# A four-layer graph kernel: empty GAT list places skipped, their factors cleared, and another pace for the tails

## The chip, the cores and the metric

The kernel runs on one core of a Trainium2 chip. The metric is the device time of one execution in microseconds (us), as the median of several runs. The kernel before took 3423.61 us (three runs, 3417.87 to 3426.96).

## The reference

Eight batches of a graph of 2,048 nodes with 128 features, and one adjacency matrix for all. Two layers of graph attention with eight heads and a feed-forward part come first, then two GAT layers. A GAT layer, shortened:

```python
h = x @ W
s_i, s_j = h @ a_src, h @ a_dst
e = s_i[:, :, None] + s_j[:, None, :]
e = jnp.where(e >= 0, e, NEG_SLOPE * e)
e = jnp.where(adj[None] == 0, -jnp.inf, e)
out = jnp.einsum('bij,bjd->bid', jax.nn.softmax(e, axis=-1), h)
x = layer_norm(out + x)
```

The adjacency has a density of 1/128, so a node has 16 neighbours on average; the inputs used have 32,733 edges, and a node has 4 to 30 of them. The kernel gathers the neighbours' rows and never forms the full score matrix.

## The kernel before

Nodes are sorted by their number of neighbours and cut into 16 tiles of 128 nodes, one node to a partition. Tile t has a list of neighbours for each node, padded to `CAPS[t]` places (28 and 2 "folded" ones for tile 0, down to 11 for tile 15; 277 in all). An empty place holds the index 2,048 (`far` in `find_lists`).

For each layer there is a table in DRAM with one row for each node. In the two attention layers (0 and 1) a row holds keys and values, 8,192 bytes. In the GAT layers (2 and 3) it holds the eight batches' features `h` and, behind them, two factors for each batch, the exponentials of `s_j` and of 0.2 `s_j`: 1,040 floats, 4,160 bytes. The GAT tables have one row more, row 2,048, which is all zeros. `gather` (L319) fetches the rows of one list place of a tile by an indirect DMA that POOL issues; an index above the bound is skipped by it. In the attention layers index 2,048 is above the bound; in the GAT layers it fetches the zero row, whose factors of zero make the place count for nothing.

The list places are worked through in chunks: two places to a chunk in the attention layers, up to four in the GAT layers (75 chunks in each). Six buffers `kv0` to `kv5` hold the gathered chunks in turn. `fetch` (L1096) issues gathers up to three or four chunks ahead, as soon as the needed part of the table has been written. `put[l]` counts the tiles whose rows are in table `l`; the first chunks of a layer use lists sorted so that they don't need the last three tiles.

A GAT chunk (`gat_chunk`, L736) works in stages: VectorE computes the weights from the two factors (L753 to L759) into PSUM and into `ws`; VectorE scales six of the eight batches (L765) and ScalarE two (L770); VectorE adds the halves of the chunk (L774); PE sums the places into `acc` (L780). When a tile has all its chunks, `outputs` divides, and a tail (`gat_tail`, or `attention_tail` in two halves) adds the residual, normalises, and projects into the next layer's rows. The squares are ScalarE's (L479, L817), the power is POOL's (L484, L844), the scaling with it is ScalarE's again (L488, L825). The rows go into the next table by an indirect scatter (`put_rows`, L502), the last layer's into the output (L862).

The order of instructions on every engine is written out by hand with Python generators. `slot()` is called three times for each chunk, and moves every list-building thread and every tail on by one stage, then calls `fetch`. In some places it moves the tails on once more:

```python
def hurry():
    c = every[min(now[0], len(every) - 1)]
    return c["l"] == 2 and c["t"] == NT - 1 or c["l"] > 1 and put[c["l"]] < NT
...
    beat[0] += 1
    if beat[0] % 3 == 0 and hurry():
        advance(tails)
```

So at every third slot there is an extra stage while the last tile of layer 2 is at work, and while a GAT layer runs whose own table isn't complete.

Of the kernel before, what the change touches and what calls it, by code (L numbers as in the profile page):

```python
# [8 lines left out]
F32 = mybir.dt.float32  # L9
# [8 lines left out]
P = 128  # L18
B, N, D = 8, 2048, 128
NT = N // P  # L20
# [8 lines left out]
NB = 8  # L29
CHUNK = 4 * NB * (D + 2)  # L30
KVB = 6
# [51 lines left out]
def sparse_path(ctx: ExitStack, tc: tile.TileContext, ins: dict, out: bass.AP, flag: bass.AP):  # L83
# [10 lines left out]
    nc = tc.nc  # L94
    const = ctx.enter_context(tc.tile_pool(name="const", bufs=1))
    work = ctx.enter_context(tc.tile_pool(name="work", bufs=2))
    small = ctx.enter_context(tc.tile_pool(name="small", bufs=2))
    dram = ctx.enter_context(tc.tile_pool(name="dram", bufs=1, space=bass.MemoryType.DRAM))
# [4 lines left out]
    def misc():  # L103
        return pm.tile([P, 512], F32, tag="m", name="m")
# [9 lines left out]
    nc.vector.tensor_scalar_add(center, ident, -1.0 / P)  # L114
    onesc = const.tile([P, 1], F32, name="onesc")
    nc.vector.memset(onesc, 1.0)
    half = const.tile([P, 8], F32, name="half")
    nc.vector.memset(half, -0.5)

# [21 lines left out]
    bufs = [const.tile([P, CHUNK], F32, name=f"kv{i}") for i in range(KVB)]  # L141
    turn = [-1]

    def buffer():
        turn[0] += 1
        return bufs[turn[0] % KVB]
# [155 lines left out]
    def width(l):  # L302
        return NB * (2 * D if l < 2 else D + 2)


    tables = [dram.tile([N + (l > 1), width(l)], F32, name=f"table{l}") for l in range(4)]

    x_rows = ins["x_nodes"]

# [9 lines left out]
    def gather(l, index, dst):  # L319
        nc.gpsimd.indirect_dma_start(  # L320
            out=dst, out_offset=None, in_=tables[l][:, :],
            in_offset=bass.IndirectOffsetOnAxis(ap=index, axis=0),
            bounds_check=N - (l < 2), oob_is_err=False,
        )

    def transpose4(src):
# [115 lines left out]
    def folded_sums(w, box):  # L442

        columns = w.shape[-1]
        ps = misc()[:, :columns]
        for i in range(FOLD):
            nc.tensor.matmul(ps, merge, w[:, i, :], start=i == 0, stop=i == FOLD - 1)
        box["folded"] = small.tile([P, columns], F32, tag="folded", name="folded", bufs=1)
        nc.scalar.copy(box["folded"], ps)
# [283 lines left out]

    def gat_chunk(l, c):  # L736
        box, t, k, ns = c["box"], c["t"], c["k"], c["ns"]
        mine = own[:, t, :]
        if c["folded"]:
            pf = misc()[:, :NB]  # L740
            nc.tensor.matmul(pf, spread, mine, start=True, stop=True)
            mine = small.tile([P, NB], F32, tag="mine", name="mine", bufs=1)
            nc.scalar.copy(mine, pf)
            yield
        if k == 0:
            box["acc"] = pacc.tile([P, NB // 4, 512], F32, tag="acc", name="acc")
            at, n = (0 if t % 2 == 0 else 512 - NB * CAPS[t]), CAPS[t]
            box["w"] = pair[:, at : at + NB * n].rearrange("p (s b) -> p s b", b=NB)
        acc, w = box["acc"], box["w"]
        hs = c["buf"]  # L750
        wc = w[:, k : k + ns, :]
        wa, wb = hs[:, :, NB * D : NB * (D + 1)], hs[:, :, NB * (D + 1) :]
        nc.vector.tensor_mul(wb, wb, mine[:, None, :].to_broadcast([P, ns, NB]))  # L753
        nc.vector.tensor_max(wc, wa, wb)
        if c["folded"]:
            box["wf"] = small.tile([P, FOLD, NB], F32, tag="wf", name="wf", bufs=1)
            nc.vector.tensor_max(box["wf"], wa, wb)
        ws = small.tile([P, 4, SCALED], F32, tag="ws", name="ws", bufs=3)
        nc.vector.tensor_max(  # L759
            ws[:, :ns, :], wa[:, :, NB - SCALED :], wb[:, :, NB - SCALED :]  # L760
        )
        yield
        hv = hs[:, :, : NB * D].rearrange("p s (b c) -> p s b c", b=NB)
        nv = NB - SCALED
        nc.vector.tensor_mul(  # L765
            hv[:, :, :nv, :], hv[:, :, :nv, :], wc[:, :, :nv, None].to_broadcast([P, ns, nv, D])
        )
        for i in range(ns):
            for b in range(nv, NB):
                nc.scalar.mul(hv[:, i, b, :], hv[:, i, b, :], ws[:, i, b - nv : b - nv + 1])  # L770
        yield
        left = -(-ns // 2)
        if ns > 1:
            nc.vector.tensor_add(hv[:, : ns - left], hv[:, : ns - left], hv[:, left:ns])  # L774
        yield
        if c["folded"]:
            folded_sums(box["wf"], box)
        for i in range(left):
            for j in range(NB // 4):
                nc.tensor.matmul(  # L780
                    acc[:, j, :], merge if c["folded"] else ident, hv[:, i, 4 * j : 4 * j + 4, :],
                    start=k + i == 0, stop=c["last"] and i == left - 1,
                )
        yield
# [85 lines left out]
    def start():  # L870
# [173 lines left out]
        next(weights, None)  # L1044
        for i in (3, 4, 5):
            nc.scalar.copy(bufs[i], nil.to_broadcast([P, CHUNK]))
        for l in (2, 3):
            nc.sync.dma_start(tables[l][N : N + 1, :], bufs[5][:1, : width(l)])


    def verdict():
# [26 lines left out]
    put = [NT, 0, 0, 0]  # L1078
    every = []
    blocks = [[{} for _ in range(NT)] for _ in range(4)]  # L1080
    for l in range(4):
        per = 2 if l < 2 else 4
        for t, k, ns, folded in pieces(l, per):
            c = dict(l=l, t=t, k=k, ns=ns, folded=folded, box=blocks[l][t])
            c["last"] = not folded and k + ns == (CAPS[t] if t > 0 else BASE)
            c["run"] = (attention_chunk if l < 2 else gat_chunk)(l, c)
            every.append(c)
    now = [0, 0]
    beat = [0]

    def advance(group):
        for g in list(group):
            if next(g, 0) == 0:
                group.remove(g)

    def fetch():  # L1096

        while now[1] < len(every):
            c = every[now[1]]
            l, t, k, ns = c["l"], c["t"], c["k"], c["ns"]  # L1100

            if now[1] - now[0] > (4 if now[1] >= KVB and every[now[1] - KVB]["l"] > 1 else 3):
                return
            resorted = l > 0 and t < 2 and not c["folded"]
            need = NT - max([b for end, b in EARLY[t] if k + ns <= end] + [0] if resorted else [0])
            if put[l] < need:
                return
            c["buf"] = buffer()[:, : ns * width(l)].rearrange("p (s c) -> p s c", s=ns)
            for i in range(ns):
                at = t * BASE if resorted else first[t]  # L1110
                index = (sorted_lists if resorted else lists)[:, at + k + i : at + k + i + 1]
                gather(l, index, c["buf"][:, i])
            now[1] += 1

    def hurry():

        c = every[min(now[0], len(every) - 1)]
        return c["l"] == 2 and c["t"] == NT - 1 or c["l"] > 1 and put[c["l"]] < NT

    def slot():  # L1120
        advance(threads)
        advance(tails)
        fetch()
        beat[0] += 1
        if beat[0] % 3 == 0 and hurry():
            advance(tails)

    def drain():
# [40 lines left out]
    def layers():  # L1169
        state(0, 0)  # L1170
        drain()
        fetch()
        begin(every[0])
        for _ in weights:
# [3 lines left out]
        for i in range(len(every) + 2):  # L1178
            now[0] = i
            fetch()  # L1180
            c2, c1, c, n1, n2 = (chunk(i + j) for j in range(-2, 3))
            if c["k"] == 0:
                l, t = c["l"], c["t"]
                if l == 0:
                    if t + 2 < NT:
                        threads.append(find_lists(t + 2))
                    if t == 0:
                        state(0, 1)
                        threads.append(later(12, lambda: state(0, 2) or iter(())))
                        threads.append(later(12, clear_late))  # L1190
                    if t in (2, 6):
                        threads.append(order_lists(t // 4))
                while l < 2 and "asked" not in c["box"]:
                    slot()
            while i < len(every) and now[1] <= i:
                slot()
# [11 lines left out]
            if c1["l"] in (2, 3) and c1["last"]:  # L1208
                sums(c1["l"], c1["t"], c1["box"])
            go(c)  # L1210
            slot()
            go(c)
            slot()
# [10 lines left out]
    with tc.manual_schedule():  # L1224
        start()
        layers()
# [521 lines left out]
```

## Time and profile before

| | |
|---|---|
| median of the runs | 3423.61 us |
| profiled execution: its own time | 3428.05 us |
| its span in the trace | 3426.3 us |
| busy PE, VectorE, ScalarE, POOL | 2761.3, 3051.6, 1425.1, 2229.1 us |
| DMA | 200,625 packets, 986.52 MB |
| first VectorE work of layer 2, first gathers of layer 3's complete table | 2223 us, 2884 us |

Busy time of an engine is the time in which it executes; a DMA instruction of POOL counts while POOL issues it, not while the data move. The DMA share is the mean busy share of the core's 16 DMA engines. A wait is put down to what ended it. In the names of groups, `kv<-table,lists` is a gather into one of the six buffers, `kv<-table,sorted_lists` the same with the sorted lists of tiles 0 and 1, and L320 is the line in `gather` that issues it.

### The profile page before, as it was taken

Reading aid. Unit: us, or ns where it says so; the run is one execution under the profiler, and the core shown is the slowest. Engines: PE = TensorE matmul, PEld = TensorE weight load, DVE = VectorE, ACT = ScalarE, POOL = GpSimd, SP = SyncE. Lnnn points to the kernel's source line nnn. Section 1 sums busy time; section 2 is a strip of 40 time slices with the busy share of each in tenths; the row PEclk is TensorE's granted clock in tenths of the full one; section 3 lists DMA queues with packets and bytes.
Section 4 is the critical chain, followed back from the end, with each engine's and each line's share of the span. In section 5 each row is a group of like instructions: output and inputs, shape, how many; then the busy total and the mean of one; then the engine's idle time right before and its main releaser. Section 6 shows DMA issues by size and latency. Waiting matters only on the chain.

```text
span 3426.3 us, 34767 instructions
## 1 busy us (share of the span) xinstructions
PE 2761.3 (81%) x10618; PEld 1595.4 (47%) x10618; DVE 3051.6 (89%) x2807; ACT 1425.1 (42%) x4972; POOL 2229.1 (65%) x1453
## 2 busy tenths in 40 slices
PE   5657888788899996888889899976888986767775
PEld 4523445455555652545455555553444543333332
DVE  8799999999999989999999999947867866889885
ACT  4712333334344441333334344453545654445444
POOL 0065888687667654566677666637767865788773
PEclk9888999999999999999999999998988998888887
DMA  8697778888878777677888888658988986899873
GB/s 326 201 355 275 284 283 303 307 303 301 312 290 296 277 287 280 238 309 284 335 298 292 315 297 295 241 171 307 326 290 311 352 326 214 291 313 334 304 275 118
DMA packets 200625, 986.52 MB, mean 288 GB/s; under 512 B 31918, under 2 KB 33712, under 8 KB 128436
## 3 DMA queue, kind: packets, MB, share of 16 engines
q0 software_dynamic: 175024, 890.45, 72.2%
q1 hardware_dynamic: 20502, 75.52, 5.9%
q10 hardware_dynamic: 4904, 18.24, 1.7%
q8 instruction: 87, 1.43, 0.2%
q14 instruction: 108, 0.88, 0.1%
HBM read 937.16 MB, written 91.55 MB: 300 GB/s over the span
## 4 chain that ended last, share of the span: by engine, by line
DVE 36%; PE 23%; issue 19%; DMA 11%; POOL 4%; ACT 4%; POOLq 0%; ACTq 0%; DVEq 0%; another core or an unknown queue 0%
DVE kv L614 13%; DVE kv L628 13%; PE acc L780 7%; PE acc L638 5%; DMA kv<-table,lists 4%; POOL kv L320 3%; DVE sc L617 3%; DMA kv<-table,sorted_lists 2%; DVE kv L774 2%; PE m L329 2%; DVE kv L765 2%; DMA table<-rows,perm 1%; DMA xs<-in_x_nodes_dram,perm 1%; PE m L720 1%; DVE w L459 1%
## 5 line engine op out<-in xcount | busy, mean ns | idle before, releaser
L320 POOL DMA_INDIRECT kv<-table,lists x955 | 1463.0, 1532 | 381.6 <-issue 203.6
L638 PE MATMUL acc<-kv,ident 128*128 128x512 f32 x2200 | 1109.0, 634 | 221.8 <-DVE kv L628 221.3
L780 PE MATMUL acc<-kv,ident 128*128 128x512 f32 x1184 | 622.2, 679 | 190.9 <-DVE kv L774 157.7
L638 PEld LDWEIGHTS acc<-kv,ident 128*128 128x128 f32 x2200 | 413.1, 201 | 652.7 <-issue 365.9
L617 DVE TENSOR_REDUCE sc<-kv 128x128 f32<-128x2048 f32 (+1 forms) x284 | 634.0, 2233 | 9.2
L628 DVE TENSOR_TENSOR kv<-kv,w 128x2048 f32<-128x2048 f32 (+1 forms) x284 | 631.5, 2223 | 8.6 <-ACT w L623 7.9
L614 DVE TENSOR_TENSOR kv<-kv,q 128x2048 f32<-128x2048 f32 (+1 forms) x282 | 629.2, 2231 | 10.7 <-DMA kv<-table,sorted_lists 5.7
L780 PEld LDWEIGHTS acc<-kv,ident 128*128 128x128 f32 x1184 | 248.9, 220 | 514.4 <-issue 294.8
L765 DVE TENSOR_TENSOR kv<-kv,pair 128x3072 f32<-128x3072 f32 (+1 forms) x150 | 466.2, 3108 | 1.0
L484 POOL TENSOR_TENSOR rs<-ss,half 128x4 f32<-128x4 f32 x128 | 222.8, 1741 | 313.9 <-ACT n L479 313.0
L774 DVE TENSOR_TENSOR kv<-kv 128x2048 f32<-128x2048 f32 (+1 forms) x150 | 296.1, 1974 | 145.9 <-ACT kv L770 137.0
L770 ACT ACTIVATE kv<-kv,ws 128x128 f32<-128x128 f32 x1108 | 339.0, 406 | 175.2 <-DVE ws L759 108.9
L479 ACT ACTIVATE n<-m,eps 128x128 f32<-128x128 f32 x512 | 181.0, 366 | 423.6 <-PE m L720 212.5
L623 ACT ACTIVATE w<-sc,lmask 128x64 f32<-128x64 f32 x554 | 165.1, 352 | 443.8 <-DVE sc L617 425.5
L320 POOL DMA_INDIRECT kv<-table,sorted_lists x153 | 203.5, 1330 | 114.8 <-PE acc L638 45.9
L488 ACT ACTIVATE n<-m,rs 128x128 f32<-128x128 f32 x512 | 146.0, 370 | 124.4 <-POOL rs L484 124.2
L502 POOL DMA_INDIRECT table<-rows,perm x57 | 102.5, 1798 | 129.1 <-ACT rows L553 33.2
L329 PE MATMUL m<-ident,n 128*128 128x128 f32 x640 | 105.2, 287 | 67.3 <-ACT n L825 47.4
L720 PE MATMUL m<-w_L_w,hT 128*128 128x128 f32 x1024 | 156.6, 275 | 1.7 <-ACT hT L704 1.7
L329 PEld LDWEIGHTS m<-ident,n 128*128 128x128 f32 x640 | 82.4, 147 | 132.6 <-ACT n L825 57.6
L720 PEld LDWEIGHTS m<-w_L_w,hT 128*128 128x128 f32 x1024 | 135.2, 192 | 1.9 <-ACT hT L704 1.9
L699 PE MATMUL m<-n1T,w_L_gnn_W 128*128 128x512 f32 x256 | 131.6, 597 | 0.8 <-ACT n1T L694 0.4
(242 smaller groups left out, 3476.4 us busy)
## 6 DMA issues: line engine op xcount, KB each, us to landing
kept<-xT SPq DMA_DIRECT2D x48, 512.0 KB
xT<-kept SPq DMA_DIRECT2D x48, 512.0 KB
kv<-in_adj_dram SPq DMA_DIRECT2D x16, 1024.0 KB
table<-kv ACTq DMA_DIRECT2D x16, 1024.0 KB
kv<-table,lists POOLq DMA_INDIRECT x955
kv<-in_x_nodes_dram SPq DMA_DIRECT2D x16, 512.0 KB
kv<-table,sorted_lists POOLq DMA_INDIRECT x153
found<-cand POOLq DMA_DIRECT2D x16, 64.0 KB
```

The source lines that it names most:

```text
L320: nc.gpsimd.indirect_dma_start(out=dst, out_offset=None, in_=tables[l][:, :], in_offset=bass.IndirectOffsetOnAxis(ap=index, axis=0), bound ...
L329: nc.tensor.transpose(pt[:, j * P : (j + 1) * P], src[:, j, :], ident)
L484: nc.gpsimd.tensor_tensor(rs, ss, half[:, :4], op=ALU.pow)
L614: nc.vector.tensor_mul(kk, kk, q[:, None].to_broadcast([P, ns, NB, D]))
L617: nc.vector.tensor_reduce(sc[:, :ns].rearrange("p s (b h) -> p (s b) h", h=NH), kk.rearrange("p s b (h j) -> p (s b) h j", h=NH), axis=AX. ...
L628: nc.vector.tensor_mul(vv, vv, w[:, k : k + ns, :].rearrange("p s (b h) -> p (s b) h", h=NH)[:, :, None, :] .to_broadcast([P, ns * NB, HD, ...
L638: nc.tensor.matmul(acc[:, j, :], merge if c["folded"] else ident, kv[:, i, 4 * j : 4 * j + 4, D:], start=k + i == 0, stop=c["last"] and i ...
L720: nc.tensor.matmul(y[:, j, :], hT[:, f, j, :], wt["2"][:, f, :], start=False, stop=f == 1, skip_group_check=True,)
L765: nc.vector.tensor_mul(hv[:, :, :nv, :], hv[:, :, :nv, :], wc[:, :, :nv, None].to_broadcast([P, ns, nv, D]))
L770: nc.scalar.mul(hv[:, i, b, :], hv[:, i, b, :], ws[:, i, b - nv : b - nv + 1])
L774: nc.vector.tensor_add(hv[:, : ns - left], hv[:, : ns - left], hv[:, left:ns])
L780: nc.tensor.matmul(acc[:, j, :], merge if c["folded"] else ident, hv[:, i, 4 * j : 4 * j + 4, :], start=k + i == 0, stop=c["last"] and i = ...
```

## The change

The gathers of the GAT layers get the same bound as the others, so an empty place moves no row; the row of zeros and its two loads go. What is then in the buffer at such a place is what the chunk before left there. So that it counts for nothing, its factors have to be zero: after a GAT chunk's scalings ScalarE writes zeros over the factors of all four places of the buffer, and for the first six chunks of layer 2, whose buffers come from an attention layer, POOL does so ahead of the gathers. Features that are left over are then multiplied by a weight of zero.

The second part is the tails' pace. There is an extra stage at every slot, but only while layer 2 is at work and its own table (`put[2]`) is incomplete; at the last tile of layer 2 and at the start of layer 3 there is none.

```diff
+    nought = const.tile([P, 1, 1], F32, name="nought")
+    nc.vector.memset(nought, 0.0)
...
-    tables = [dram.tile([N + (l > 1), width(l)], F32, name=f"table{l}") for l in range(4)]
+    tables = [dram.tile([N, width(l)], F32, name=f"table{l}") for l in range(4)]
...
-            bounds_check=N - (l < 2), oob_is_err=False,
+            bounds_check=N - 1, oob_is_err=False,
...
+    def gat_weights(buf):
+        return buf[:, : 4 * width(2)].rearrange("p (s c) -> p s c", s=4)[:, :, NB * D :]
...
                 nc.scalar.mul(hv[:, i, b, :], hv[:, i, b, :], ws[:, i, b - nv : b - nv + 1])
+        nc.scalar.copy(gat_weights(c["whole"]), nought.to_broadcast([P, 4, 2 * NB]))
         yield
...
-        for l in (2, 3):
-            nc.sync.dma_start(tables[l][N : N + 1, :], bufs[5][:1, : width(l)])
...
-            c["buf"] = buffer()[:, : ns * width(l)].rearrange("p (s c) -> p s c", s=ns)
+            c["whole"] = buffer()
+            c["buf"] = c["whole"][:, : ns * width(l)].rearrange("p (s c) -> p s c", s=ns)
+            if l == 2 and every[now[1] - KVB]["l"] == 1:
+                nc.gpsimd.memset(gat_weights(c["whole"]), 0.0)
...
-    def hurry():
-        c = every[min(now[0], len(every) - 1)]
-        return c["l"] == 2 and c["t"] == NT - 1 or c["l"] > 1 and put[c["l"]] < NT
...
-        beat[0] += 1
-        if beat[0] % 3 == 0 and hurry():
+        if now[0] < len(every) and every[now[0]]["l"] == 2 and put[2] < NT:
             advance(tails)
```

More of the change, by code (lines that the diff above doesn't have):

```diff
@@ L1088, in sparse_path @@
     now = [0, 0]
-    beat = [0]
     def advance(group):
```

## The prediction

> **What bounds the kernel now.** I read the busy shares by stage first, then the groups of the two GAT layers, then who waited for whom there, then the DMA counts. The first chunk of the third layer starts on VectorE at 2223 us and the program ends at 3426 us, so the change can act on some 1,206 us. Busy time in five stretches (columns: length, PE, PEld, DVE, ACT, POOL with their counts, PE clock, DMA share, GB/s):
>
> ```profile
> 2220.00:2320.00 100.00, 70.17 (x327) 44.68 (x325) 47.59 (x45) 45.25 (x171) 39.77 (x36) 0.89 0.50 166
> 2320.00:2795.00 475.00, 398.47 (x1408) 222.37 (x1408) 385.49 (x412) 248.92 (x969) 349.59 (x272) 0.89 0.91 322
> 2795.00:2890.00 95.00, 64.50 (x250) 38.45 (x250) 48.43 (x46) 41.25 (x163) 47.73 (x37) 0.82 0.62 214
> 2890.00:3350.00 460.00, 321.86 (x786) 145.90 (x787) 388.41 (x415) 202.78 (x775) 357.30 (x263) 0.85 0.88 304
> 3350.00:3426.00 76.00, 41.47 (x121) 20.89 (x119) 43.68 (x56) 25.98 (x110) 22.43 (x16) 0.79 0.29 100
> ```
>
> The second and fourth are the bodies of layers 2 and 3 (counted from 0). In both the DMA engines are the fullest resource: 0.91 x 475 = 432 us against PE 398 and DVE 385; 0.88 x 460 = 405 us against DVE 388. The lead is small, 34 and 17 us. The first and third are the changes of layer, where all is half idle. The groups (busy time and mean ns after the first bar), then the waits from 2220 us on (us in total, times, longest):
>
> ```profile
> L770 ACT ACTIVATE kv<-kv,ws 128x128 f32<-128x128 f32 x1108 | 339.0, 406 | 175.2 <-DVE ws L759 108.9
> L623 ACT ACTIVATE w<-sc,lmask 128x64 f32<-128x64 f32 x554 | 165.1, 352 | 443.8 <-DVE sc L617 425.5
> L878 POOL MEMSET kv<- 128x64 f32 x3 | 0.3, 141 | 0.0
> ```
>
> ```profile
> DVE kv L774 <- ACT kv L770: 137.0, 32, 11.1
> ACT rows L817 <- DMA out_dram<-rows,perm: 110.2, 12, 15.8
> DVE kv L753 <- DMA kv<-table,lists: 36.0, 5, 23.9
> ```
>
> VectorE hardly waits for a gather itself: 36.0 us in five waits, 23.9 of them the one at 2300 to 2324 us. It waits for ScalarE (137.0 us), and ScalarE waits for the output scatter of the tile before (110.2 us), which stands in the DMA queue behind gathers, or for the power on POOL, which stands behind them too. So the DMA load reaches VectorE by way of ScalarE. The counts:
>
> ```profile
> DMA packets 200625, 986.52 MB, mean 288 GB/s; under 512 B 31918, under 2 KB 33712, under 8 KB 128436
> q0 software_dynamic: 175024, 890.45, 72.2%
> ```
>
> **What the Trainium skill says.** "DMA: Bandwidth & Descriptors", section "The descriptor swizzle": each DMA engine writes a fixed set of partitions. If that also holds for a gather, rows left out save unequal time; no view here shows the engines singly. "ScalarE: Activation LUTs", "Rules for kernel authors": some 0.3 us for an instruction plus 0.83 ns an element, 0.35 us for 64; L623 shows 352 ns, so it agrees. "Perfetto Trace Analysis", the section on TensorE instructions, adds that ScalarE, VectorE and GpSimd queues are strictly first in, first out; the waits of L770 behind tails agree.
>
> **The change part by part.**
>
> *Skipped rows.* The adjacency of the inputs has 32,733 edges and the lists have 277 x 128 = 35,456 places, so 2,723 places in a layer are empty. Before, each of them in a GAT layer reads a row of zeros, 4,160 B; after, an index of 2,048 is out of bounds and no row moves. That this works is seen in the attention layers, which do so already: 200,625 - 128,436 = 72,189 packets have 8 KB or more, which is exactly 2 x 32,733 gathered rows, 19 x 128 scattered ones, 2,048 rows of table 0, 2,048 of the adjacency and the 195 packets of the instruction queues. So 5,446 packets and 22.65 MB go. At the body's full rate, 322/0.91 = 354 GB/s, one layer saves 11.33 MB or 32 us of DMA time. POOL issues the same 554 gathers as before (some 1.0 us and a gap of 0.3 us where nothing holds it), so nothing is gained there.
>
> What of it reaches the end: 749 of the 2,723 lie in tile 0, whose chunks come first in a layer, 241 of them in the two gathers of the folded chunk. The first wait ends with a folded gather that takes 6.2 us; if it lands at once, the chunk behind it, already issued, ends the wait: 3 us a layer, **-6 us** (0 to -12). The other 1,974 are worth 23 us a layer on average. The nodes of a tile are sorted by degree, so empty places lie on high partitions. By the skill's map the engine with the fewest loses 117 of 2,216 rows (5.3%), the one with the most 241 (10.9%); the fullest engine then gains about 0.7 of the average, 16 us. VectorE and PE take over soon: in layer 2 I count 13 us (PE is 34 us away), in layer 3 DMA falls from 405 to some 385 us, below VectorE's 388, and I count 9. Together **-22 us** (0 to -50; more than all DMA time can't go).
>
> *Clearing the factors.* 150 copies of 128x64 on ScalarE, one after each chunk's scalings (L770). No row shows this copy; the nearest is L623 at 352 ns, two of which in a row take 0.59 us in the timeline, so 0.24 us each in the queue and 36 us in all. They wait for nothing that the scalings did not wait for (VectorE has read the factors), and the next gather into that buffer waits longer for PE. Behind a copy stands a tail's work or the next chunk's scalings. Cover: ScalarE is busy 249 of 475 and 203 of 460 us. The cover fails where VectorE waits for L770: 32 of 150 chunks, 32/150 x 36 = **+8 us** (0 to +36). Six POOL memsets in the first chunks of layer 2 cost 141 ns each by L878, **+1 us** with the gathers behind them.
>
> *Tails at the start of layer 2.* The instruction order before and after has the same VectorE and PE work; ScalarE and POOL change. Before, an extra stage comes at each third slot, after at each slot. The last tile's scatter now stands behind six chunks' scalings and not seven, which takes one chunk's 2.4 us off its ScalarE path. But POOL now has all four powers of the last tile behind the eight gathers of 2270 to 2282 us, where one was ahead: some 4 us more until the second power, which waits for what ScalarE does with the first. The scatter ahead of those gathers (2265 us) waited for a landing, and still does. **0 us** (-10 to +10).
>
> *Tails from layer 2 to 3.* The extra stages at the last tile go. POOL gets the power of tile 14 ahead of the scatter of tile 13, that of tile 15 ahead of that of tile 14; before, each stood behind a scatter that waited 5 to 8 us for data, and ScalarE waited up to 13.3 us for the power. Against that the scatter of tile 14 now waits for the last tile's sums. If this loses, the scatter of tile 15 (2879 us) is late next. **0 us** (-10 to +10).
>
> *The rest.* Two loads of the zero row on SP's queue and one more 1-column memset on VectorE at the start, under the preparation: 0; if the cover were gone, under 1 us.
>
> Sum: -6 - 22 + 8 + 1 = **-19 us**. Against the profiled execution's own 3428.05 us (span 3426.3) that is 3409; the median of the runs is 4.4 us below that execution, so I forecast **3405 us**.
>
> **The rivals.** *DMA is the whole pace.* For it: 0.91 and 0.88, gathers of 3 us on POOL instead of 1.0 where the queue is full, 110.2 us of waits for a scatter in the queue. Against it: PE and VectorE at 84% of the bodies. If 26 us a layer are gained and the copies stay in ScalarE's idle time: 3424 - 52 = about 3372. *Nothing arrives.* VectorE, PE and the order between them set the bodies, and skipped rows only lengthen DMA's idle time; the copies cost what the starts give back: about 3422. *ScalarE becomes the pace (slower).* Place: its queue in the bodies, where a chunk's scalings stand behind tails and now behind a copy too, and VectorE's addition (L774) waits for them. Price: up to 36 us in the bodies, plus tails pushed ahead of scalings at the start of layer 2. If 30 us are exposed and 6 us come from the skips: 3448. It decides once a copy exposes more than 28/150 = 0.19 us a chunk. For it: 137.0 us of such waits now; against it: ScalarE is half idle. *The gathers don't skip:* excluded by the packet count above.
>
> **How the numbers follow.** Likeliest case (-8 to -32 us, 3392 to 3416): 0.45. DMA the pace (3350 to 3392): 0.17. Nothing arrives (3414 to 3434): 0.15. ScalarE (above 3434): 0.23. About 0.3% (10 us) is what a measurement here can tell from no change; a little of the first case lies inside it, so faster 0.60, same 0.17, slower 0.23. The range, 3365 to 3450, leaves out the far ends of the second and fourth case.
>
> **What would show it.** Packets 195,180 and 964 MB. The copy as a new ScalarE group x150 at about 0.25 to 0.35 us. DMA share in the bodies near 0.87 with shorter bodies; the waits for the output scatter under 110 us; L774's waits for L770 not above 137. I am wrong if the bodies keep their length with a lower DMA share (nothing arrives), if L774's waits grow (ScalarE), or if the stretches between layers move by over 10 us.

## The result, and the profile after

The kernel after took 3400.82 us (median of five runs, 3394.65 to 3405.46), the kernel before 3419.58 us on the same chip (five runs). The ratio is 0.994, with a 95% interval of 0.9924 to 0.9955: 19 us less by the medians, 15 to 26 us by the interval. The forecast was 3405 us.

The profiled execution of after has a span of 3393.1 us, 33 us below that of before. That is more than the medians differ by; 4.6 us of it lie ahead of the first chunk of layer 2, where the change does nothing, so the two profiles show where time went but not how much in all.

The page of after, DMA part (packets and bytes of the whole program, then of POOL's queue):

```profile
DMA packets 200621, 963.87 MB, mean 284 GB/s; under 512 B 37362, under 2 KB 39156, under 8 KB 128432
q0 software_dynamic: 175024, 867.82, 71.2%
```

22.65 MB are gone, as forecast. The number of packets is not down: 5,444 more of them have under 512 bytes. In the traces the packets of 4,160 bytes fell from 75,776 to 70,330, and those of 4 bytes rose from 25,926 to 31,372, both by 5,446, twice the 2,723 empty places of a layer. A skipped row leaves a packet of 4 bytes in place of a full one.

The same five stretches as in the prediction, cut at the same chunks (columns: length, PE, PEld, DVE, ACT, POOL, PE clock, DMA share, GB/s):

```profile
2215.00:2309.00 94.00, 72.61 (x328) 45.62 (x326) 47.77 (x46) 46.98 (x179) 39.54 (x38) 0.87 0.50 170
2309.00:2781.00 472.00, 396.38 (x1408) 220.57 (x1408) 385.02 (x412) 257.99 (x1035) 353.67 (x276) 0.90 0.87 302
2781.00:2859.00 78.00, 57.56 (x244) 35.78 (x245) 48.50 (x46) 41.97 (x170) 39.70 (x34) 0.87 0.70 248
2859.00:3320.00 461.00, 325.52 (x795) 147.36 (x794) 388.06 (x415) 212.07 (x841) 358.51 (x266) 0.85 0.83 283
3320.00:3393.00 73.00, 41.39 (x121) 20.70 (x119) 43.58 (x56) 26.72 (x115) 22.33 (x16) 0.80 0.25 86
```

The bodies, second and fourth, kept their lengths (472 against 475, 461 against 460 us) while their DMA share fell from 0.91 to 0.87 and from 0.88 to 0.83. The stretches between the layers got shorter: 94 against 100 us, and 78 against 95. How much of that is due to which part of the change, the experiments below tell. Of the groups and waits of after, those that answer to the ones shown of before (groups from the GAT layers on ScalarE, waits from 2200 us on):

```profile
L775 ACT ACTIVATE kv<-kv,ws 128x128 f32<-128x128 f32 x1108 | 341.0, 405 | 167.3 <-DVE ws L764 91.2 <-PE acc L787 38.5 <-issue 26.0
L777 ACT COPY kv<-nought 128x64 f32<-128x64 f32 x150 | 36.2, 242 | 0.0
```

```profile
DVE kv L781 <- ACT kv L775: 123.7, 30, 18.6
ACT rows L824 <- DMA out_dram<-rows,perm: 105.2, 11, 15.2
DVE kv L758 <- DMA kv<-table,lists: 24.2, 9, 8.7
DVE kv L758 <- DMA kv<-table,sorted_lists: 24.4, 7, 10.6
```

Before, VectorE's waits for gathers with the sorted lists were these:

```profile
DVE kv L753 <- DMA kv<-table,sorted_lists: 16.3, 9, 8.0
```

L777 is the new copy. VectorE's waits for gathers of both kinds are 48.6 us after and were 52.3 before: the long wait of 23.9 us is gone, but most of its time stands elsewhere. ScalarE still waits 105.2 us (110.2 before) for output scatters to land, though the DMA queue has less in it.

Between layers 2 and 3 the two timelines of POOL show the order that the prediction had described and priced at nothing. First before, from 2828 us, then after, from 2807 us (start, duration, line, idle time ahead and what ended it); gathers are left out, "..." stands for them:

```profile
2828.39 1.01 POOL L502 DMA_INDIRECT table<-rows,perm  x1 [7.81 <-DMA kv<-table,sorted_lists]
2829.42 1.67 POOL L844 TENSOR_TENSOR rs<-ss,half 128x8 f32<-128x8 f32 x1
...
2844.51 2.33 POOL L502 DMA_INDIRECT table<-rows,perm  x1 [5.44 <-ACT rows L553]
...
2863.82 1.68 POOL L844 TENSOR_TENSOR rs<-ss,half 128x8 f32<-128x8 f32 x1
2878.80 2.36 POOL L502 DMA_INDIRECT table<-rows,perm  x1 [13.30 <-ACT score L555]
```

```profile
2807.82 1.66 POOL L851 TENSOR_TENSOR rs<-ss,half 128x8 f32<-128x8 f32 x1 [4.83 <-ACT n L824]
2811.82 1.43 POOL L503 DMA_INDIRECT table<-rows,perm  x1 [2.34 <-DMA kv<-table,sorted_lists]
...
2828.86 1.68 POOL L851 TENSOR_TENSOR rs<-ss,half 128x8 f32<-128x8 f32 x1 [6.21 <-ACT kv L775]
2830.74 1.06 POOL L503 DMA_INDIRECT table<-rows,perm  x1 [0.20 <-issue]
...
2853.09 1.02 POOL L503 DMA_INDIRECT table<-rows,perm  x1 [7.79 <-DMA kv<-table,sorted_lists]
```

Before, the last tile's power (2863.82) stood behind the scatter of tile 14, the landing of that scatter and eight gathers; its rows were scattered at 2878.80. After, it comes ahead of the scatter of tile 14, and its tail runs while the eight gathers are issued and land. From the scatter of tile 13 to that of tile 15 it is 50.4 us before and 41.3 us after. Skips have little part in this step: in the kernel with skips and the old pace (below) it is 50.3 us, in the one with the late half of the new pace and no skips 42.1 us, with the powers in the same places as in after.

### The profile page after: what moved, and what is told of

It is laid out like the page before. It is cut to its first block, busy times and chain, and to the rows that moved or that the text cites. A ratio compares the mean times of both kernels' runs of the same rounds, so it can differ in the third digit from the quotient of the medians.

```text
span 3393.1 us, 34890 instructions
## 1 busy us (share of the span) xinstructions
PE 2753.5 (81%) x10618; PEld 1591.4 (47%) x10618; DVE 3050.4 (90%) x2808; ACT 1447.6 (43%) x5122; POOL 2214.9 (65%) x1459
## 2 busy tenths in 40 slices
DMA packets 200621, 963.87 MB, mean 284 GB/s; under 512 B 37362, under 2 KB 39156, under 8 KB 128432
## 4 chain that ended last, share of the span: by engine, by line
DVE 36%; PE 23%; issue 20%; DMA 8%; POOL 5%; ACT 4%; another core or an unknown queue 0%; POOLq 0%; DVEq 0%; ACTq 0%; SPq 0%
DVE kv L629 12%; DVE kv L615 12%; PE acc L787 7%; PE acc L639 5%; POOL kv L321 4%; DVE sc L618 3%; DVE kv L781 2%; DVE kv L770 2%; DMA kv<-table,sorted_lists 2%; DMA kv<-table,lists 2%; PE m L330 1%; PE m L721 1%; DMA table<-rows,perm 1%; DVE w L460 1%; DMA out_dram<-rows,perm 1%
## 5 line engine op out<-in xcount | busy, mean ns | idle before, releaser
L770 DVE TENSOR_TENSOR kv<-kv,pair 128x3072 f32<-128x3072 f32 (+1 forms) x150 | 466.1, 3108 | 1.0
L485 POOL TENSOR_TENSOR rs<-ss,half 128x4 f32<-128x4 f32 x128 | 213.5, 1668 | 327.7 <-ACT n L480 326.8
L503 POOL DMA_INDIRECT table<-rows,perm x57 | 94.4, 1657 | 111.3 <-DMA kv<-table,sorted_lists 19.8
```

The lines of the kernel that those rows point to most:

```text
L485: nc.gpsimd.tensor_tensor(rs, ss, half[:, :4], op=ALU.pow)
L770: nc.vector.tensor_mul(hv[:, :, :nv, :], hv[:, :, :nv, :], wc[:, :, :nv, None].to_broadcast([P, ns, nv, D]))
```

## The experiments

Each kernel was compared with the kernel before on one chip. The kernel before took 3394 to 3420 us on the chips used, so ratios are given, and "us" are worked out from the medians of one comparison. Beside the ratios I use stretches cut at the start of VectorE's scaling (L765; L770 after the change) of chunks 0, 7 (the folded one of layer 2), 74 (the last of layer 2), 82 (the folded one of layer 3) and 149 (the last), from the timeline of each kernel's one profiled execution:

| kernel | 0 to 7 | 7 to 74 | 74 to 82 | 82 to 149 |
|---|---|---|---|---|
| before | 100.5 | 471.8 | 98.0 | 487.6 |
| after | 93.8 | 469.3 | 81.2 | 484.9 |
| skips, old pace | 95.8 | 448.5 | 91.7 | 487.8 |
| pace only | 94.9 | 445.0 | 86.2 | 487.1 |
| clearing only | 97.7 | 445.3 | 95.9 | 487.9 |
| after, no clearing | 93.6 | 448.0 | 82.6 | 487.0 |
| late pace only | 98.5 | 464.0 | 86.9 | 486.8 |
| early pace only | 98.1 | 463.5 | 95.6 | 486.1 |
| after again | 93.8 | 470.1 | 82.6 | 488.3 |
| fourth place skipped | 92.2 | 462.7 | 78.8 | 476.9 |
| half sums on PE | 88.3 | 442.8 | 81.9 | 485.9 |
| after, two outputs | 92.2 | 448.7 | 81.1 | 452.9 |
| before, two outputs | 99.2 | 446.1 | 94.3 | 452.1 |
| two outputs, late scale | 94.7 | 449.8 | 83.4 | 445.3 |

The second column differs between chips more than between kernels ("skips, old pace" to "after, no clearing" are of one chip, "late pace only" to "fourth place skipped" of another, "half sums on PE" and "after, two outputs" of a third, "before, two outputs" and the last row of a fourth), so it is compared on one chip only; the last column hardly differs.

### The parts of the change

Skips and clearing, with before's `hurry` and every third slot (against after):

```diff
...
-        if now[0] < len(every) and every[now[0]]["l"] == 2 and put[2] < NT:
+        beat[0] += 1
+        if beat[0] % 3 == 0 and hurry():
             advance(tails)
```

> The skipped rows and the clearing of the factors, with the tails' pace as it was before. Theory 'layer changes' (the gain of 19 us lies mostly in the two changes of layer, above all in the tails' pace between layers 2 and 3, and the bodies do not follow the DMA load): about 8 us below before, 3412 us. Rival 'DMA load' (the gain is the bytes that no longer move): 18 us or more below before, 3402 us or less.

Measured: 0.9986 (0.9978 to 0.9995), 5 us less. The theory of the layer changes was nearer, and even it was too high. On the chip of this run the body of layer 2 is no shorter than without skips (448.5 against 445.0 and 445.3 us), that of layer 3 is the same; 74 to 82 is some 4 us shorter than with the rows of zeros. In layer 2 as a whole, from chunk 0 to 74, the skips bring nothing: 544.3 us with them and 543.0 without at the old pace, 541.6 and 539.9 at the new one, and on another chip 563.9 against 561.6 and 562.5. What they save at its start is gone by its last chunk.

The pace alone, before's kernel with after's `slot`:

```diff
...
-        beat[0] += 1
-        if beat[0] % 3 == 0 and hurry():
+        if now[0] < len(every) and every[now[0]]["l"] == 2 and put[2] < NT:
             advance(tails)
```

> The tails' new pace alone; empty places still fetch the row of zeros and nothing is cleared. 'Layer changes': about 11 us below before, 3408 us, with the folded chunk of layer 3 some 12 us earlier against the folded chunk of layer 2. 'DMA load': within 4 us of before.

Measured: 0.9971 (0.9961 to 0.9981), 11 us less. The stretch 74 to 82 is 86.2 us, 9.7 below "clearing only" of the same chip. Fewer bytes had no part in it.

The clearing alone, before's kernel with the copies and memsets of the diff:

```diff
...
+        nc.scalar.copy(gat_weights(c["whole"]), nought.to_broadcast([P, 4, 2 * NB]))
...
+            if l == 2 and every[now[1] - KVB]["l"] == 1:
+                nc.gpsimd.memset(gat_weights(c["whole"]), 0.0)
```

> The 150 clearings on ScalarE and the six on POOL alone; empty places still fetch the row of zeros, pace as before. The prediction's term: 8 us above before, 3428 us. Rival (the copies fit into ScalarE's idle time; the trace after shows the next instruction 0.13 us behind a copy, 150 x 0.13 = 20 us of its queue): within 3 us of before.

Measured: 0.9998 (0.9988 to 1.0008). The copies cost nothing that shows, and the interval ends at 3 us. And the other way round, after without copies and memsets:

```diff
-        nc.scalar.copy(gat_weights(c["whole"]), nought.to_broadcast([P, 4, 2 * NB]))
...
-            if l == 2 and every[now[1] - KVB]["l"] == 1:
-                nc.gpsimd.memset(gat_weights(c["whole"]), 0.0)
```

> The kernel after, without any clearing of the factors, so that left-over factors at empty places are counted; skips and pace as after. If a copy costs what the prediction says: 8 us below after, 3393 us. If the copies are covered: within 3 us of after, 3398 to 3404 us.

Measured: 0.9947 (0.9934 to 0.996) against before; after itself was at 0.994 and 0.9952 on other chips. Nothing that shows is gained by leaving the clearing out.

The two halves of the pace, each on before's kernel. In the first, `hurry` holds only at the start of layer 2; in the second, the start of layer 2 gets a stage at every slot and the rest stays:

```diff
-        return c["l"] == 2 and c["t"] == NT - 1 or c["l"] > 1 and put[c["l"]] < NT
+        return c["l"] == 2 and put[2] < NT
```

```diff
-        return c["l"] == 2 and c["t"] == NT - 1 or c["l"] > 1 and put[c["l"]] < NT
+        return c["l"] == 2 and c["t"] == NT - 1 or c["l"] > 2 and put[c["l"]] < NT
...
+        if now[0] < len(every) and every[now[0]]["l"] == 2 and put[2] < NT:
+            advance(tails)
```

> Of the new pace only the late half: no extra stage at the last tile of layer 2 and the start of layer 3; at the start of layer 2 the extra stage comes at each third slot as before. Rows of zeros fetched, nothing cleared. Theory 'POOL order' (between layers 2 and 3 the powers of tiles 14 and 15 now stand ahead of scatters that wait for data): the whole of the pace's gain, 10 to 14 us below before. Rival (the gain is in the denser tails at the start of layer 2, or shared equally): 5 us or less below.

> Of the new pace only the early half: an extra stage at each slot at the start of layer 2; between layers 2 and 3 as before. Rows of zeros fetched, nothing cleared. 'POOL order': between 4 us above and 2 us below before, since the powers of the last tile get behind eight gathers. Rival: 5 us or more below.

Measured: late half 0.9977 (0.9967 to 0.9988), 9 us less; early half 0.9994 (0.9983 to 1.0006), 1 us less (6 less to 2 more), not to be told from nothing. The late half came out a little below its 10 to 14 us, with 74 to 82 at 86.9 against 95.6 us; the interval's end is 4 us, so the ratio alone does not exclude the rival's 5 us; the stretch does. That the early half brings nothing was expected.

The whole change beside them:

> The whole change beside its halves on one chip. If its parts add up (skips with clearing 0.14%, pace 0.29%): 0.43% below before, some 15 us. If they help each other, as the first measurement of 0.6% would have it: 18 us or more below.

Measured: 0.9952 (0.9936 to 0.9967), 17 us less. The parts give 0.43%, inside this interval, though just short of that of the first measurement (0.45 to 0.76%). With some 0.1% of uncertainty on each part, they add up within the noise; a joint effect of a few us is neither seen nor excluded.

### Why the bodies do not follow

A much larger cut of the DMA load: the fourth place of every chunk of four is out of bounds for all nodes.

```diff
+    absent = const.tile([P, 1], I32, name="absent")
+    nc.vector.memset(absent, N)
...
-                gather(l, index, c["buf"][:, i])
+                gather(l, absent if l > 1 and i == 3 else index, c["buf"][:, i])
```

> After, but in both GAT layers the fourth place of every chunk of four gets an index out of bounds for all nodes, so 106 of 554 gathers move no row and the neighbours there are left out of the result. All other work is the same. If the bodies follow the DMA load: 19% of 430 us in each layer is 80 us, of which VectorE and PE let through 25 or more: 50 us below after. If VectorE, PE and ScalarE set the bodies: 15 us or less below after.

Measured: 0.99 (0.9883 to 0.9917) against before, 17 us below after on the same chip. The bodies of this kernel (same columns as above):

```profile
2310.00:2770.00 460.00, 388.85 (x1398) 215.83 (x1397) 378.68 (x406) 255.18 (x1025) 353.26 (x275) 0.90 0.79 260
2860.00:3320.00 460.00, 332.09 (x821) 151.78 (x822) 399.26 (x426) 215.06 (x849) 363.68 (x268) 0.86 0.75 243
```

The DMA share falls to 0.79 and 0.75, and the bodies get 7 and 11 us shorter than in "after again". 12,308 rows beyond after's empty places, 51 MB, bought 17 us: a little above the 15 that the second case allowed, and far from the 50 that were expected if the bodies followed the DMA load. A DMA share of 0.9 was not the pace.

Once more on the kernel after, with PE summing only half of each chunk in layer 2:

```diff
-        for i in range(left):
+        for i in range(1 if l == 2 else left):
...
-                    start=k + i == 0, stop=c["last"] and i == left - 1,
+                    start=k + i == 0, stop=c["last"] and i == (0 if l == 2 else left - 1),
```

> After, but PE sums only the first half of every chunk's added places in layer 2 (two matrix products of 128x512 for a full chunk and not four); the other half is left out of layer 2's result. VectorE, ScalarE, POOL and the DMAs do the same work. Theory 'PE paces the body of layer 2' (377 us busy of 440, and the body is shorter where the granted clock is higher): some 130 us of PE's work go and the body gets shorter until VectorE and DMA stop it, 30 us or more below after. Rival 'VectorE and ScalarE pace it': 8 us or less below after.

Measured: 0.993 (0.9915 to 0.9946) against before. After was not run on this chip; against its ratios of 0.994 and 0.9952 that is 3 to 7 us. The body of layer 2 is 442.8 us, against 448.7 us of the next kernel, which has all sums, on the same chip. In the middle of the body (first this kernel, then the next) PE is busy for 53 us less of 300, at a lower clock:

```profile
2400.00:2700.00 300.00, 206.55 (x816) 119.05 (x816) 260.18 (x276) 181.44 (x734) 243.10 (x186) 0.83 0.93 333
2400.00:2700.00 300.00, 259.47 (x991) 145.19 (x990) 258.17 (x271) 178.42 (x716) 242.14 (x185) 0.95 0.93 329
```

PE does not set the body there. But this chip has the short body and the high clock (0.98 from 2450 to 2600 us in the next kernel). Where before and after were measured, the body is longer and the clock lower (0.87 and 0.86), and there the half sums were not tried.

After, with two buffers for layer 3's output rows, which so far lie in the one `rows` tile. The tag `q` has two buffers that only the attention layers use, so no memory is added:

```diff
-            n = rows_of(box)[:, : B * D].rearrange("p (b d) -> p b d", d=D)
+            n = work.tile([P, NB, D], F32, tag="q", name="n3")
```

> After, with layer 3's normalised rows in two buffers that layer 3 does not use otherwise, so that ScalarE's squares need not wait until the output scatter of the tile before has landed. Theory 'the scatter paces layer 3' (97 us of such waits in ten or so places): layer 3 gets 20 us or more shorter, and the kernel with it. Rival 'those waits are ScalarE's idle time, VectorE's 385 us of 460 set the pace': 8 us or less below after.

Measured: 0.9839 (0.9821 to 0.9856), 57 us below before on its chip, where after had been 17 to 19 below. Layer 3 from 82 to 149 takes 452.9 us, 32 less than after. In after, two waits in layer 3 (2860 to 3320 us) were these:

```profile
ACT rows L824 <- DMA out_dram<-rows,perm: 79.2, 8, 15.2
DVE kv L781 <- ACT kv L775: 32.9, 6, 8.2
```

With two buffers neither is in the lists of the same stretch, and 32.9 us is about what the layer lost. The body at the same place as after's fourth stretch:

```profile
2859.00:3320.00 461.00, 344.11 (x882) 160.04 (x883) 417.67 (x454) 230.57 (x915) 356.67 (x265) 0.87 0.83 285
```

VectorE is busy 418 of 461 us, against 388 of after. So ScalarE's squares stood in its queue until a landing, chunk scalings stood behind them, and VectorE's additions waited for those.

The same edit on the kernel before:

> Before, with layer 3's normalised rows in two buffers as in the kernel just measured. If the scatter's landing is a fixed price of layer 3: some 35 us below before, 1.0%, as the two buffers brought after. If the skips matter only once that wait is gone (DMA becomes the pace of layer 3): 25 us or less below before, 0.75%, since the fuller DMA queue takes a part.

Measured: 0.9887 (0.9871 to 0.9902), 39 us. Layer 3 takes 452.1 us, as with skips. So the wait was a fixed price of layer 3, the skips do not matter in the body even with it gone, and the 0.48% between the two kernels is what the change brings elsewhere.

Last, after with two outputs and a longer way between the power and its use in layer 3:

```diff
-        for _ in range(3):
+        for _ in range(6 if l == 3 else 3):
             yield
```

> After with two output buffers, and in layer 3 six slots and not three between the power on POOL and the scaling on ScalarE that needs it, so that ScalarE stands less behind a power that is behind gathers (77 us of such waits were left). If those waits reach VectorE: 8 us or more below the kernel with two buffers alone, 1.9% below before or more. If they are idle time: within 4 us of it, 1.5 to 1.75% below before. The last tile's tail gets three slots longer, up to 4 us at the end.

Measured: 0.9823 (0.9803 to 0.9843). Layer 3 is 445.3 us, 7 below that of two outputs alone, but the intervals of the two ratios overlap, so whether it adds anything is open. Both beat the kernels before and after.

## Why the prediction was right

The total was right, 19 us forecast and 17 to 19 measured, but by luck: three large terms were wrong and their errors cancelled. By the prediction's own signs its mechanism failed: the bodies kept their length at a lower DMA share, and the stretch from layer 2 to 3 moved by more than 10 us.

- **Skips at the starts, -6 us:** half right. The step from 74 to 82, with the start of layer 3, is 4 us shorter with skips at either pace (91.7 against 95.9, 82.6 against 86.9), where 3 were forecast. In layer 2 the wait for the first folded gather fell from 23.9 to 8.7 us in the profile, but from chunk 0 to 74 nothing was gained. Skips with clearing measured 5 us in all.
- **Skips in the bodies, -22 us: the step that failed.** I took the resource with the largest busy share, 0.91, for the pace and let two thirds of its saving through. The bodies gave nothing: no shorter on the chips where both were run. (One figure of that working was off too: by the map that it used and the inputs' degrees, the engine with the fewest empty places loses 109 rows and not 117, which changes its gain by about 1 us.) In layer 3 the pace was a chain through one buffer: square, power, scale, scatter, landing, next square. The wait stood in the profile (110.2 us) and in my text, but I read it as a wait for a loaded queue, which a lighter load would shorten. It went to 105.2 us; a second buffer removed it, and 32 us of the layer with it. In layer 2 the DMA load is not the pace (7 us for a further 19% of the gathered rows on a chip with the long body, nothing for the skips on one with the short body), and PE is not on the one chip where it was tried (6 us for half its sums); which chain is, stays open. A chain through `rows` as in layer 3 does not show there. Between 2330 and 2760 us of "after again", ScalarE's largest sum of waits is for POOL's power, and it waits once for a scatter into the table:

```profile
ACT n L832 <- POOL rs L851: 59.1, 12, 10.2
ACT rows L550 <- DMA table<-rows,perm: 7.3, 1, 7.3
```

  No run took these waits for the power out of layer 2.
- **The packet count** of 195,180 was wrong: a skipped row stays as a packet of 4 bytes. The bytes were right.
- **Clearing, +8 us:** it measured 0 within 4, at most 3 of cost. L777 lasts 242 ns, but the timeline of ScalarE has the next instruction start 0.13 us after it, half of the 0.24 us that I had taken, and where ScalarE was late in layer 3, most of the delay came from one wait and not from its work.
- **Tails at the start of layer 2, 0 us:** right as far as can be told, -1 us (-6 to +2). VectorE's longest wait for scalings did grow, from 11.1 to 18.6 us, at 2279 us, and "early pace only" has the same wait (18.7 us) without being slower.
- **Tails from layer 2 to 3, 0 us (-10 to +10):** it measured -9 (-11 to -4), inside the range. The step between the scatters of tiles 13 and 15 shrank by 8 to 9 us with the new order of POOL, with skips and without; that the place of the two powers alone does it is read from the timelines, since the late half moves other stages of the tails too. I had described the order and set it off against a scatter that would have to wait for the last tile's sums. That scatter did go out at 2830.74 us with 0.20 us of waiting, behind a power that had waited 6.21 us, and what was gained behind it was more.
- **The rival "nothing arrives"** was right on the bodies, and "ScalarE becomes the pace" had the place in part: VectorE did wait for ScalarE's queue in layer 3, but for a wait that was there before and not for the copies.

## What to carry to other kernels

A resource at 0.9 busy is not yet the pace: look for a chain that passes through a single buffer and back, and count what a landing costs there, before pricing a lighter load. On an in-order queue the place of a short instruction ahead of one that waits for data can be worth more than megabytes: here 9 us went with two powers moved ahead of scatters, against 5 us with 22.65 MB less. A wait that shrinks at one place may only have moved: compare the time at the end of the layer. When a sum comes out right, measure its terms all the same.

## What the runs showed of the hardware

- A row that an indirect gather skips still counts as a packet, one of 4 bytes: 200,621 packets against 200,625, with 5,446 more of 4 bytes and 5,446 fewer of 4,160.
- The body of layer 2 took 442.8 to 449.8 us or 462.7 to 471.8 us, by chip; before and after of the first two rows are among the long ones. In the stretch of 2450 to 2600 us, before was granted a mean PE clock of 0.87 and "clearing only", which has the same PE work in the layer, on another chip, 0.97:

```profile
2450.00:2600.00 150.00, 124.83 (x427) 70.03 (x426) 112.96 (x126) 75.31 (x292) 97.94 (x81) 0.87 0.86 299
```

```profile
2450.00:2600.00 150.00, 130.96 (x492) 72.27 (x493) 131.78 (x144) 90.70 (x366) 119.54 (x94) 0.97 0.96 353
```

  Whether the clock makes the body shorter or goes along with something else was not tried. With half of PE's sums left out, the mean clock was 0.84 in this stretch and the body was short all the same, so the low clock by itself did not make it long there. This is why lengths of this body are compared on one chip only.
